# The last image's layers 2 and 3 written beside the end of the last but one's layer 3

## The chip, the cores and the metric

The kernel runs on one core of a Trainium2 chip. A core has TensorE (PE, matrix products into PSUM; its weight loads are shown as PEld), VectorE (DVE), ScalarE (ACT), GpSimd (POOL) and SyncE (SP), which issues most of the DMAs. Each engine works off its own queue. The metric is the device time of one execution in microseconds. Before the change it was 3833.54 us, the median of 3 runs (3829.8 to 3834.8).

## The reference, cut to what matters

Four residual layers run one after the other over x of shape (8, 384, 32, 32), each on a group-normalised input. All arithmetic is in f32.

```python
x = x + L0(_gn(x))   # depthwise 3x3, batch norm, attention with 8 heads
x = x + L1(_gn(x))   # 4 experts, top 2 routing, 384 -> 384 -> 384
x = x + L2(_gn(x))   # depthwise 3x3 with ternary weights, then 1x1 with ternary weights
x = x + L3(_gn(x))   # deformable attention, 6 heads
```

Layer 3 on one image:

```python
q = einsum('bchw,oc->bohw', x, q_w)
off = gelu(bn(conv5x5_stride2(q, groups=128)))         # depthwise, 3 groups of 128 channels
offset, modulation = 1x1(off)                          # tanh, sigmoid
x_s = grid_sample_bilinear(x, positions) * modulation  # 16 x 16 samples per group
k, v = einsum(x_s, kv_w)
out = softmax(q k^T / 8) v                             # 1024 queries, 256 keys
out = einsum(out, proj_w) + proj_b
```

From layer 1 on no image depends on another one. The layers of one image depend on each other.

## The kernel before, in words

An image is held as a tile of 128 partitions x 3 channel slices x 1024 pixels in f32 (`image`, five buffers). Layer 0 takes the first half of the run and isn't touched. The rest works image by image. `layer1` returns a list of 48 units, 24 for each half of 512 pixels: 12 hidden units (`hidden`, L1232: three products, a ReLU on ScalarE into a tile `hd0` to `hd11` at L1240, and a weighting on VectorE at L1218), then 12 output units (`result`, L1251), each of which adds the products of three hidden tiles into a bank. The fourth part of an output slice adds the bank to the image (L1257).

`layer2` and `layer3` are generators. They write out instructions, and at each `yield` they tell how long, in microseconds by the author's estimate, TensorE would have nothing to do. The loop at the end of the kernel sums these numbers and, whenever they reach `UNIT` (2.6), writes out one unit of the next image's layer 1:

```python
for stage in (layer2(pl, b, xt), layer3(pl, b, xt, put_image(b), False)):
    for idle in stage:
        due += idle
        while due >= UNIT and units:
            units.pop(0)()
            due -= UNIT
for u in units:
    u()
```

For the last image there are no units, so its layers 2 and 3 are written after all of the last but one's. The programming framework plans each engine's queue from what is written: what is written earlier goes first, but an instruction whose inputs are ready can go ahead of one that is still waiting. Once planned, a queue is worked off in its order.

`layer2` takes statistics (`gn_start`, L105), normalises them with two small products and a power on GpSimd (`gn_finish`, L116 to L132), applies them on ScalarE (`affine`, L146, into `h2`), and runs the 3x3 depthwise convolution as nine taps per channel slice (L1311 the first, L1320 the others) on VectorE. On the last image slice 0 runs on GpSimd instead (L1311, L1323, L1324: product into a temporary, then a sum). The 1x1 convolution is `pw` (L1341, 36 matmuls), added to the image at L1345 and stored at L1346.

`layer3` normalises again into `h3`, computes q (`pq`, L1367; copied out at L76 or L78 by turns of ScalarE and VectorE), transposes `h3` (`px`, L1379, copied into `xT`), runs the 5x5 convolution with stride 2 on VectorE (`off`, L1413 and L1415) and a GELU (L1420). Then come the offsets (`pom`, L1426 and L1427; L1430 to L1445), bilinear weights for eight row blocks (L1458 to L1460, the last on GpSimd) and sampling products (`xsb`, `xs`, L1464, L1471), k and v (`pk`, `pv`, L1478, L1487), six attention units (scores `s` L1504, exponentials L1511, pair sum on GpSimd L1535, `pav` L1520, `pss` L1546, and VectorE's transposes, reciprocal and product L1538 to L1557), and the projection (`pf`, L1609, added at L1613, stored at L1620).

[...]`big` is two tiles of two banks (pw, pq, px, pom, scores, projection), `vbank` is one bank (statistics, `xs2`, pav, pss), `fbank` is three single banks (layer 1).

Of the kernel before, what the change touches and what calls it, by code (L numbers as in the profile page):

```python
# [9 lines left out]
ALU = mybir.AluOpType  # L10
AX = mybir.AxisListType

B, C, H, W = 8, 384, 32, 32
N = H * W
P = 128
# [37 lines left out]
def tile_kernel(ctx: ExitStack, tc: tile.TileContext, i: dict, out: bass.AP):  # L53
# [10 lines left out]
    def big(name):  # L64
        return ps_big.tile([P, N], F32, tag="big", name=name)
# [71 lines left out]
    def gn_finish(st, tag, psum):  # L137

        return gn_scale(*gn_spread(gn_mean(st, tag), tag, psum), tag, psum)
# [5 lines left out]
    def affine(dst, src, ss):  # L145
        nc.scalar.activation(dst, src, AF.Identity, bias=ss[:, 1:2], scale=ss[:, 0:1])  # L146
# [1006 lines left out]

    xs_img, started = {}, {}

    def layer1(pl, b, late=False):


# [69 lines left out]
        def hidden(h, k):  # L1228
            e, dc = divmod(k, KC)
            ph = fbank(f"ph{b}_{h}_{k}")  # L1230
            for c in range(KC):
                nc.tensor.matmul(  # L1232
                    ph, lhsT=w1[:, e, c, dc * P : (dc + 1) * P], rhs=state["h1"][c],
                    start=(c == 0), stop=(c == KC - 1),
                )
            if late and h == 1:
                hd = spare(k)
            else:
                hd = pl.one([P, HALF], f"hd{k}", f"hd{b}_{h}_{k}")
# [56 lines left out]
        return units  # L1296

    def layer2(pl, b, xt):
        st = None
        for c in range(KC):  # L1300
            st = gn_start(xt, f"d2_{b}", c, st)
            yield 1.3
        ss = gn_finish(st, f"d2_{b}", vbank)
        yield 5.0
        h2, y = pl.img(f"h2_{b}"), pl.img(f"y_{b}")
        for c in range(KC):
            affine(h2[:, c, :], xt[:, c, :], ss)
        def taps(c, eng):
            src = h2[:, c, :].rearrange("p (h w) -> p h w", h=H)
            dst = y[:, c, :].rearrange("p (h w) -> p h w", h=H)  # L1310
            eng.tensor_scalar(dst, src, tap2[:, c, 4:5], None, ALU.mult)  # L1311
            yield 0.8
            for t in (0, 1, 2, 3, 5, 6, 7, 8):
                dy, dx = t // 3 - 1, t % 3 - 1
                r0, r1 = max(0, -dy), H - max(0, dy)
                c0, c1 = max(0, -dx), W - max(0, dx)
                d = dst[:, r0:r1, c0:c1]
                f = src[:, r0 + dy : r1 + dy, c0 + dx : c1 + dx]
                if eng is nc.vector:
                    eng.scalar_tensor_tensor(d, f, tap2[:, c, t : t + 1], d, ALU.mult, ALU.add)  # L1320
                else:
                    tmp = pl.flat([P, r1 - r0, c1 - c0], f"tap{t}_{b}")
                    eng.tensor_scalar(tmp, f, tap2[:, c, t : t + 1], None, ALU.mult)  # L1323
                    eng.tensor_tensor(d, d, tmp, ALU.add)  # L1324
                yield 1.25


        alone = b == B - 1
        for c in range(KC):
            if alone and c == 0:  # L1330
                for _ in taps(c, nc.gpsimd):
                    pass
            else:
                yield from taps(c, nc.vector)
        yield 2.0
        for m in range(KC):
            pw = big(f"pw{b}_{m}")
            for h in range(2):
                hs = slice(h * HALF, (h + 1) * HALF)
                for c in range(KC):  # L1340
                    nc.tensor.matmul(  # L1341
                        pw[:, hs], lhsT=upw2[:, c, m * P : (m + 1) * P], rhs=y[:, c, hs],
                        start=(c == 0), stop=(c == KC - 1),
                    )
            nc.vector.scalar_tensor_tensor(xt[:, m, :], pw, mp, xt[:, m, :], ALU.mult, ALU.add)  # L1345
            nc.sync.dma_start(out=x2_dram[b, :, m, :], in_=xt[:, m, :])  # L1346
            yield 0.0

    def layer3(pl, b, xt, put, general):

        st = None
        for c in range(KC):
            st = gn_start(xt, f"d3_{b}", c, st)
        yield 3.0
        ss = gn_finish(st, f"d3_{b}", vbank)
        yield 5.0
        h3 = pl.img(f"h3_{b}")
        for c in range(KC):
            affine(h3[:, c, :], xt[:, c, :], ss)
        yield 3.0  # L1360
        q = pl.img(f"q_{b}")
        for m in range(KC):
            pq = big(f"pq3_{b}_{m}")
            for h in range(2):
                hs = slice(h * HALF, (h + 1) * HALF)
                for c in range(KC):
                    nc.tensor.matmul(  # L1367
                        pq[:, hs], lhsT=wq3[:, c, m * P : (m + 1) * P], rhs=h3[:, c, hs],
                        start=(c == 0), stop=(c == KC - 1),
                    )  # L1370
            evac(q[:, m, :], pq)
            yield 0.0

        xT = pl.img(f"xT_{b}").rearrange("p c n -> p (c n)").rearrange("p (t c) -> p t c", t=NT8)
        for t in range(0, NT8, 2):
            px = big(f"px_{b}_{t}")
            for k in range(2):
                for c in range(KC):
                    nc.tensor.transpose(  # L1379
                        px[:, k * HALF + c * P : k * HALF + (c + 1) * P],  # L1380
                        h3[:, c, (t + k) * P : (t + k + 1) * P], ident,
                    )
            evac(
                xT[:, t : t + 2, :].rearrange("p t (q c) -> p t c q", c=KC),
                px.rearrange("p (t n) -> p t n", t=2)[:, :, :C].rearrange(
                    "p t (c q) -> p t c q", c=KC
                ),
            )
            yield 0.4

        off = pl.flat([P, NG, HS, HS], f"off_{b}")
        src = q.rearrange("p g (h w) -> p g h w", h=H)

        def span(s):
# [24 lines left out]
        offf = off.rearrange("p g h w -> p (g h w)")  # L1419
        nc.scalar.activation(offf, offf, AF.Gelu, bias=bo3, scale=so3)  # L1420
        yield 3.0

        om = []
        for r in range(3):
# [29 lines left out]
        for t in range(NT8):  # L1454
            i0, i1 = _sample_rows(t)
            sl = slice(i0 * HS, i1 * HS)
            wt = pl.flat([P, NG, (i1 - i0) * HS], f"wt_{b}_{t}")
            nc.scalar.activation(wt, gy3[:, :, sl], AF.Abs, bias=npos[:, t : t + 1])  # L1458
            nc.scalar.activation(wt, wt, AF.Relu, bias=1.0, scale=-1.0)
            nc.gpsimd.tensor_tensor(wt, wt, gx3[:, :, sl], ALU.mult)  # L1460
            if t == 0:
                yield 2.0
            for g in range(NG):
                nc.tensor.matmul(  # L1464
                    xps[g][:, sl], lhsT=xT[:, t, g * P : (g + 1) * P], rhs=wt[:, g, :],
                    start=False, stop=(t == NT8 - 1), skip_group_check=True,
                )
            yield 0.5
# [150 lines left out]
    def put_image(b):  # L1619
        return lambda m, xt: nc.sync.dma_start(out=out_img[b][:, m, :], in_=xt[:, m, :])  # L1620
# [23 lines left out]
    with pd:  # L1644
        for k, u in enumerate(units):
            u()
            if k == 8:
                tap2, upw2, mp, so3, bo3 = weights23(pl)
        for b in range(B):
            xt = xs_img.pop(b)  # L1650
            units = layer1(pl, b + 1) if b + 1 < B else []
            due = 0.0
            for stage in (layer2(pl, b, xt), layer3(pl, b, xt, put_image(b), False)):
                for idle in stage:
                    due += idle
                    while due >= UNIT and units:
                        units.pop(0)()
                        due -= UNIT
# [166 lines left out]
```

## Time and profile before

| what | us |
|---|---|
| median of 3 runs | 3833.54 |
| the profiled execution | 3834.06 |
| its span, first to last instruction | 3832.2 |
| TensorE busy in it | 3646.2 |
| VectorE busy in it | 1823.4 |
| GpSimd busy in it | 235.5 |
| mean granted TensorE clock | 0.975 |

Times in the views below are microseconds from the span's start unless marked ns. A line of groups or of waits names line, engine and tiles ("pw L1341 <- POOL y L1324" is a wait of the product pw for GpSimd's writing of y). The row of slices divides the span into 40 parts of 96 us; a digit is the busy share in tenths, and PEclk the granted clock in tenths of full speed. Matmuls of f32 show as two records each, so one unit of layer 1 is six.

### The profile page before, as it was taken

Reading aid. Unit: us, or ns where it says so; the run is one execution under the profiler, and the core shown is the slowest. Engines: PE = TensorE matmul, PEld = TensorE weight load, DVE = VectorE, ACT = ScalarE, POOL = GpSimd, SP = SyncE. Lnnn points to the kernel's source line nnn. Section 1 sums busy time; section 2 is a strip of 40 time slices with the busy share of each in tenths; the row PEclk is TensorE's granted clock in tenths of the full one; section 3 lists DMA queues with packets and bytes.
Section 4 is the critical chain, followed back from the end, with each engine's and each line's share of the span. In section 5 each row is a group of like instructions: output and inputs, shape, how many; then the busy total and the mean of one; then the engine's idle time right before and its main releaser. Section 6 shows DMA issues by size and latency. Waiting matters only on the chain.

```text
span 3832.2 us, 39353 instructions
## 1 busy us (share of the span) xinstructions
PE 3646.2 (95%) x15754; PEld 1520.9 (40%) x15754; DVE 1823.4 (48%) x2826; ACT 1314.7 (34%) x1557; POOL 235.5 (6%) x170
## 2 busy tenths in 40 slices
PE   7999899999999999999899999999999999999748
PEld 3444333333333333333344445444444444445213
DVE  5876223232323232332256665475656646565544
ACT  2222454554546353534112323223232222313102
POOL 0000000000000000000000100101011010100321
PEclk9999999999999999999899999999999999999868
DMA  6777211121202121111620000101001010010000
GB/s 200 245 235 241 100 53 43 53 61 40 74 24 72 27 69 38 59 49 50 233 81 33 17 33 19 48 17 33 33 17 34 17 50 17 25 42 1 17 17 18
DMA packets 83097, 242.64 MB, mean 63 GB/s; under 512 B 18336, under 2 KB 18864, under 8 KB 82520
## 3 DMA queue, kind: packets, MB, share of 16 engines
q1 hardware_dynamic: 69894, 200.56, 15.7%
q10 hardware_dynamic: 13008, 39.43, 3.0%
q8 instruction: 128, 2.10, 0.2%
q14 instruction: 67, 0.55, 0.0%
HBM read 122.78 MB, written 75.50 MB: 52 GB/s over the span
## 4 chain that ended last, share of the span: by engine, by line
PE 39%; DVE 9%; POOL 1%; issue 1%; ACT 1%; DVEq 0%; ACTq 0%; POOLq 0%
PE y L1251 10%; PE ph L1232 8%; DVE y L1320 5%; PE pq L1367 3%; PE pw L1341 3%; PE s L1504 3%; PE pf L1609 3%; PE pav L1520 2%; PE pss L1546 1%; DVE hd L1218 1%; DVE off L1415 1%; PE pk L1478 1%; PE xsb L1464 1%; PE pv L1487 1%; POOL tap L1323 1%
## 5 line engine op out<-in xcount | busy, mean ns | idle before, releaser
L630 ACT ACTIVATE p<-s 128x1024 f32<-128x1024 f32 x512 | 496.4, 1021 | 497.1 <-PE s L623 496.8
L1251 PE MATMUL y<-hd,w_sb 128*128 128x512 f32 x1080 | 493.4, 601 | 3.6 <-DVE hd L1218 3.6
L638 PE MATMUL pav<-p,vt 64*64 64x512 f32 x4096 | 486.4, 589 | 0.0
L1232 PE MATMUL ph<-h,w_sb 128*128 128x512 f32 x1104 | 483.6, 594 | 0.0
L623 PE MATMUL s<-qk,qk 48*64 48x512 f32 x3072 | 373.1, 600 | 4.4 <-ACT p L630 4.4
L381 PE MATMUL pk<-st,cw_sb 126*126 126x512 f32 x720 | 321.5, 608 | 3.6 <-DVE ga_a L118 3.3
L1232 PEld LDWEIGHTS ph<-h,w_sb 128*128 128x128 f32 x1104 | 207.8, 190 | 252.5 <-issue 249.4
L1251 PEld LDWEIGHTS y<-hd,w_sb 128*128 128x128 f32 x1080 | 198.8, 191 | 250.4 <-issue 236.3
L638 PEld LDWEIGHTS pav<-p,vt 64*64 64x64 f32 x4096 | 156.2, 133 | 285.3 <-issue 285.0
L595 DVE COPY ta<-pav 128x512 f32<-128x512 f32 x64 | 44.3, 692 | 439.1 <-PE pav L638 436.1
L1320 DVE SCALAR_TENSOR_TENSOR y<-h,tap,y 128x961 f32<-128x961 f32 (+1 forms) x184 | 233.5, 1295 | 1.6
L381 PEld LDWEIGHTS pk<-st,cw_sb 126*126 126x126 f32 x720 | 140.1, 197 | 177.7 <-issue 170.7
L1415 DVE SCALAR_TENSOR_TENSOR off<-q,dw_sb,off 128x225 f32<-128x225 f32 (+3 forms) x432 | 209.6, 542 | 1.9
L1240 ACT ACTIVATE hd<-ph,b_sb 128x512 f32<-128x512 f32 x180 | 122.6, 681 | 254.3 <-PE ph L1232 253.9
L623 PEld LDWEIGHTS s<-qk,qk 48*64 48x64 f32 x3072 | 102.6, 133 | 241.6 <-issue 184.7
L1341 PE MATMUL pw<-y,upw 128*128 128x512 f32 x288 | 128.6, 602 | 54.8 <-POOL y L1324 50.1
L78 DVE COPY qk<-pq 128x512 f32<-128x512 f32 x48 | 33.2, 692 | 293.1 <-PE pq L558 281.4
L387 ACT COPY y<-pk 126x512 f32<-126x512 f32 (+1 forms) x136 | 76.2, 583 | 254.4 <-DMA raw<-y 115.9
L1511 ACT ACTIVATE p<-s 128x1024 f32<-128x1024 f32 x96 | 93.0, 1021 | 171.8 <-PE s L1504 171.7
L146 ACT ACTIVATE h<-x,ss_d 128x1024 f32<-128x1024 f32 x42 | 49.6, 1231 | 287.6 <-DVE ss_d L132 287.6
L575 PE MATMUL po<-att,wo_sb 128*128 128x512 f32 x288 | 134.5, 617 | 9.5 <-DMA att<-al 9.5
L1218 DVE TENSOR_TENSOR hd<-hd,cb 128x512 f32<-128x512 f32 x180 | 122.9, 688 | 34.6 <-ACT hd L1240 34.2
(281 smaller groups left out, 4124.0 us busy)
## 6 DMA issues: line engine op xcount, KB each, us to landing
g<-raw SPq DMA_DIRECT2D x72, 512.0 KB
st<-pad SPq DMA_DIRECT2D x180, 168.0 KB
raw<-y ACTq DMA_DIRECT2D x180, 168.0 KB
xa<-in_x_dram SPq DMA_DIRECT2D x24, 512.0 KB
xh<-in_x_dram SPq DMA_DIRECT2D x48, 256.0 KB
f<-in_x_dram SPq DMA_DIRECT2D x24, 512.0 KB
f<-o SPq DMA_DIRECT2D x24, 512.0 KB
o<-ot SPq DMA_DIRECT2D x42, 256.0 KB
```

The source lines that it names most:

```text
L381: nc.tensor.matmul(pk[h].rearrange("p (h w) -> p h w", w=W)[: 3 * nch, :, o0 : o0 + c1 - c0], lhsT=lhs, rhs=rhs, start=(k == 0), stop=(k = ...
L575: nc.tensor.matmul(po, lhsT=wo0[:, c, m * P : (m + 1) * P], rhs=atts[b][:, c, hs], start=(c == 0), stop=(c == KC - 1),)
L623: nc.tensor.matmul(s[64 * k : 64 * k + 64, j * HALF : (j + 1) * HALF], lhsT=kt[r, k0 : k0 + 64], rhs=qt[r, h * HALF : (h + 1) * HALF], sta ...
L630: nc.scalar.activation(p, s, AF.Exp, scale=scale)
L638: nc.tensor.matmul(pav[k][64 * j : 64 * j + 64, :], lhsT=vts[b % 2][r, kc, 2 * hd : 2 * hd + 2, :].rearrange("p a b -> p (a b)"), rhs=p[r, ...
L1218: nc.vector.tensor_tensor(hd, hd, state["cb"], ALU.mult)
L1232: nc.tensor.matmul(ph, lhsT=w1[:, e, c, dc * P : (dc + 1) * P], rhs=state["h1"][c], start=(c == 0), stop=(c == KC - 1),)
L1240: nc.scalar.activation(hd, ph, AF.Relu, bias=b1[:, k : k + 1])
L1251: nc.tensor.matmul(y, lhsT=w2[:, e, dc, m * P : (m + 1) * P], rhs=state[h, k], start=(k == 0), stop=(k == NE * KC - 1),)
L1320: eng.scalar_tensor_tensor(d, f, tap2[:, c, t : t + 1], d, ALU.mult, ALU.add)
L1341: nc.tensor.matmul(pw[:, hs], lhsT=upw2[:, c, m * P : (m + 1) * P], rhs=y[:, c, hs], start=(c == 0), stop=(c == KC - 1),)
L1415: nc.vector.scalar_tensor_tensor(d, f, dw3[:, t : t + 1], d, ALU.mult, ALU.add)
```

## The change

The loop stops following the old scheme in the last but one image (image 6; the last is image 7). `layer3` gets a marker, `yield None`, right after the GELU of the offsets. At this marker in image 6 all remaining units of image 7's layer 1 are written out at once. Then the rest of image 6's layer 3 and the whole of image 7's layers 2 and 3 are written in turn: after each step of image 6, two steps of image 7. In the other images the marker does nothing.

For image 7 the tiles and banks are others: statistics, pw, pq and px use the three `fbank` banks in halves of 512 (or 384), where the other images use `big` and `vbank`; `y`, `h3` and `xT` lie in the tiles of layer 1's hidden values, and `off` in the tile `h1`. For this the twelve tiles `hd0` to `hd11` become four tiles of three slices each, in all images. The copies out of these banks, the affine into `h3` and the sums into the image are done in halves. The convolution of image 7's layer 2 has all three slices on VectorE.

```diff
+    def third(pl, k, name):
+        return pl.one([P, KC, HALF], f"hd{k}", name)
+
+    def pair(last, name):
+        if last:
+            return None, [fbank(f"{name}_{h}") for h in range(2)]
+        t = big(name)
+        return t, [t[:, :HALF], t[:, HALF:]]
...
-                hd = pl.one([P, HALF], f"hd{k}", f"hd{b}_{h}_{k}")
+                if k % 3 == 0:
+                    state["hd"] = third(pl, k // 3, f"hd{b}_{h}_{k}")
+                hd = state["hd"][:, k % 3, :]
...
     def layer2(pl, b, xt):
+        last = b == B - 1
...
-        ss = gn_finish(st, f"d2_{b}", vbank)
+        ss = gn_finish(st, f"d2_{b}", fbank if last else vbank)
...
+        if last:
+            y = [third(pl, c, f"y_{b}_{c}").rearrange("p a n -> p (a n)")[:, :N] for c in range(KC)]
...
-        alone = b == B - 1
-        for c in range(KC):
-            if alone and c == 0:
-                for _ in taps(c, nc.gpsimd):
-                    pass
-            else:
-                yield from taps(c, nc.vector)
...
-            pw = big(f"pw{b}_{m}")
+            whole, pw = pair(last, f"pw{b}_{m}")
...
+            outs = zip((xm[:, :HALF], xm[:, HALF:]), pw) if last else [(xm, whole)]
+            for d, f in outs:
+                nc.vector.scalar_tensor_tensor(d, f, mp, d, ALU.mult, ALU.add)
...
     def layer3(pl, b, xt, put, general):
...
+        if last:
+            h3 = [third(pl, h, f"h3_{b}_{h}") for h in range(2)]
+            for h in range(2):
+                for c in range(KC):
+                    affine(h3[h][:, c, :], xt[:, c, h * HALF : (h + 1) * HALF], ss)
...
+            whole, pq = pair(last, f"pq3_{b}_{m}")
...
+            if last:
+                for h in range(2):
+                    evac(q[:, m, h * HALF : (h + 1) * HALF], pq[h])
...
+            xT = [third(pl, 2 + h, f"xT_{b}_{h}").rearrange("p a n -> p (a n)") for h in range(2)]
...
+            off = pl.one([P, KC, HALF], "h1", f"off_{b}").rearrange("p c n -> p (c n)")
...
         nc.scalar.activation(offf, offf, AF.Gelu, bias=bo3, scale=so3)
         yield 3.0
+
+        yield None
...
+        def layers(b):
             xt = xs_img.pop(b)
+            yield from layer2(pl, b, xt)
+            yield from layer3(pl, b, xt, put_image(b), False)
+
+        for b in range(B - 1):
+            units = layer1(pl, b + 1)
             due = 0.0
+            this = layers(b)
+            for idle in this:
+                if idle is None:
+                    if b == B - 2:
+                        break
+                    continue
+                due += idle
+                while due >= UNIT and units:
+                    units.pop(0)()
+                    due -= UNIT
             for u in units:
                 u()
+
+        following = layers(B - 1)
+        for _ in this:
+            for _ in range(2):
+                next(following)
+        for _ in following:
+            pass
```

More of the change, by code (lines that the diff above doesn't have):

```diff
@@ L1302, in layer2 @@
             yield 1.3
-        ss = gn_finish(st, f"d2_{b}", vbank)
+        ss = gn_finish(st, f"d2_{b}", fbank if last else vbank)
         yield 5.0
-        h2, y = pl.img(f"h2_{b}"), pl.img(f"y_{b}")
+        h2 = pl.img(f"h2_{b}")
+        if last:
+            y = [third(pl, c, f"y_{b}_{c}").rearrange("p a n -> p (a n)")[:, :N] for c in range(KC)]
+        else:
+            y = pl.img(f"y_{b}")
+            y = [y[:, c, :] for c in range(KC)]
         for c in range(KC):
             affine(h2[:, c, :], xt[:, c, :], ss)
-        def taps(c, eng):
+        for c in range(KC):
             src = h2[:, c, :].rearrange("p (h w) -> p h w", h=H)
-            dst = y[:, c, :].rearrange("p (h w) -> p h w", h=H)
-            eng.tensor_scalar(dst, src, tap2[:, c, 4:5], None, ALU.mult)
+            dst = y[c].rearrange("p (h w) -> p h w", h=H)
+            nc.vector.tensor_scalar(dst, src, tap2[:, c, 4:5], None, ALU.mult)
             yield 0.8
@@ L1318, in taps @@
                 f = src[:, r0 + dy : r1 + dy, c0 + dx : c1 + dx]
-                if eng is nc.vector:
-                    eng.scalar_tensor_tensor(d, f, tap2[:, c, t : t + 1], d, ALU.mult, ALU.add)
-                else:
-                    tmp = pl.flat([P, r1 - r0, c1 - c0], f"tap{t}_{b}")
-                    eng.tensor_scalar(tmp, f, tap2[:, c, t : t + 1], None, ALU.mult)
-                    eng.tensor_tensor(d, d, tmp, ALU.add)
-                yield 1.25
-        alone = b == B - 1
-        for c in range(KC):
-            if alone and c == 0:
-                for _ in taps(c, nc.gpsimd):
-                    pass
-            else:
-                yield from taps(c, nc.vector)
+                nc.vector.scalar_tensor_tensor(d, f, tap2[:, c, t : t + 1], d, ALU.mult, ALU.add)
+                yield 1.25
         yield 2.0
         for m in range(KC):
-            pw = big(f"pw{b}_{m}")
+            whole, pw = pair(last, f"pw{b}_{m}")
             for h in range(2):
@@ L1341, in layer2 @@
                     nc.tensor.matmul(
-                        pw[:, hs], lhsT=upw2[:, c, m * P : (m + 1) * P], rhs=y[:, c, hs],
+                        pw[h], lhsT=upw2[:, c, m * P : (m + 1) * P], rhs=y[c][:, hs],
                         start=(c == 0), stop=(c == KC - 1),
                     )
-            nc.vector.scalar_tensor_tensor(xt[:, m, :], pw, mp, xt[:, m, :], ALU.mult, ALU.add)
-            nc.sync.dma_start(out=x2_dram[b, :, m, :], in_=xt[:, m, :])
+            xm = xt[:, m, :]
+            outs = zip((xm[:, :HALF], xm[:, HALF:]), pw) if last else [(xm, whole)]
+            for d, f in outs:
+                nc.vector.scalar_tensor_tensor(d, f, mp, d, ALU.mult, ALU.add)
+            nc.sync.dma_start(out=x2_dram[b, :, m, :], in_=xm)
             yield 0.0
     def layer3(pl, b, xt, put, general):
+        last = b == B - 1
         st = None
@@ L1354, in layer3 @@
         yield 3.0
-        ss = gn_finish(st, f"d3_{b}", vbank)
+        ss = gn_finish(st, f"d3_{b}", fbank if last else vbank)
         yield 5.0
-        h3 = pl.img(f"h3_{b}")
-        for c in range(KC):
-            affine(h3[:, c, :], xt[:, c, :], ss)
+        if last:
+            h3 = [third(pl, h, f"h3_{b}_{h}") for h in range(2)]
+            for h in range(2):
+                for c in range(KC):
+                    affine(h3[h][:, c, :], xt[:, c, h * HALF : (h + 1) * HALF], ss)
+        else:
+            t = pl.img(f"h3_{b}")
+            for c in range(KC):
+                affine(t[:, c, :], xt[:, c, :], ss)
+            h3 = [t[:, :, :HALF], t[:, :, HALF:]]
         yield 3.0
@@ L1362, in layer3 @@
         for m in range(KC):
-            pq = big(f"pq3_{b}_{m}")
+            whole, pq = pair(last, f"pq3_{b}_{m}")
             for h in range(2):
-                hs = slice(h * HALF, (h + 1) * HALF)
                 for c in range(KC):
                     nc.tensor.matmul(
-                        pq[:, hs], lhsT=wq3[:, c, m * P : (m + 1) * P], rhs=h3[:, c, hs],
+                        pq[h], lhsT=wq3[:, c, m * P : (m + 1) * P], rhs=h3[h][:, c, :],
                         start=(c == 0), stop=(c == KC - 1),
                     )
-            evac(q[:, m, :], pq)
-            yield 0.0
-        xT = pl.img(f"xT_{b}").rearrange("p c n -> p (c n)").rearrange("p (t c) -> p t c", t=NT8)
+            if last:
+                for h in range(2):
+                    evac(q[:, m, h * HALF : (h + 1) * HALF], pq[h])
+            else:
+                evac(q[:, m, :], whole)
+            yield 0.0
+        T2 = NT8 // 2
+        if last:
+            xT = [third(pl, 2 + h, f"xT_{b}_{h}").rearrange("p a n -> p (a n)") for h in range(2)]
+        else:
+            t = pl.img(f"xT_{b}").rearrange("p c n -> p (c n)")
+            xT = [t[:, : T2 * C], t[:, T2 * C :]]
+        xT = [t.rearrange("p (t c) -> p t c", t=T2) for t in xT]
         for t in range(0, NT8, 2):
-            px = big(f"px_{b}_{t}")
+            h, t2 = divmod(t, T2)
+            whole, px = pair(last, f"px_{b}_{t}")
             for k in range(2):
@@ L1379, in layer3 @@
                     nc.tensor.transpose(
-                        px[:, k * HALF + c * P : k * HALF + (c + 1) * P],
-                        h3[:, c, (t + k) * P : (t + k + 1) * P], ident,
-                    )
[L1383 to L1388, printed above, removed]
-            yield 0.4
-        off = pl.flat([P, NG, HS, HS], f"off_{b}")
+                        px[k][:, c * P : (c + 1) * P],
+                        h3[h][:, c, (t2 + k) * P : (t2 + k + 1) * P], ident,
+                    )
+            if last:
+                for k in range(2):
+                    evac(
+                        xT[h][:, t2 + k, :].rearrange("p (q c) -> p c q", c=KC),
+                        px[k][:, :C].rearrange("p (c q) -> p c q", c=KC),
+                    )
+            else:
+                evac(
+                    xT[h][:, t2 : t2 + 2, :].rearrange("p t (q c) -> p t c q", c=KC),
+                    whole.rearrange("p (t n) -> p t n", t=2)[:, :, :C].rearrange(
+                        "p t (c q) -> p t c q", c=KC
+                    ),
+                )
+            yield 0.4
+        if last:
+            off = pl.one([P, KC, HALF], "h1", f"off_{b}").rearrange("p c n -> p (c n)")
+            off = off[:, : NG * LS].rearrange("p (g h w) -> p g h w", g=NG, h=HS)
+        else:
+            off = pl.flat([P, NG, HS, HS], f"off_{b}")
         src = q.rearrange("p g (h w) -> p g h w", h=H)
@@ L1464, in layer3 @@
                 nc.tensor.matmul(
-                    xps[g][:, sl], lhsT=xT[:, t, g * P : (g + 1) * P], rhs=wt[:, g, :],
+                    xps[g][:, sl], lhsT=xT[t // T2][:, t % T2, g * P : (g + 1) * P], rhs=wt[:, g, :],
                     start=False, stop=(t == NT8 - 1), skip_group_check=True,
@@ L1648, in tile_kernel @@
                 tap2, upw2, mp, so3, bo3 = weights23(pl)
-        for b in range(B):
+        def layers(b):
             xt = xs_img.pop(b)
-            units = layer1(pl, b + 1) if b + 1 < B else []
+            yield from layer2(pl, b, xt)
+            yield from layer3(pl, b, xt, put_image(b), False)
+        for b in range(B - 1):
+            units = layer1(pl, b + 1)
             due = 0.0
[L1653 to L1658, printed above, removed]
+            this = layers(b)
[8 more added lines that the diff above has]
+                    due -= UNIT
             for u in units:
                 u()
+        following = layers(B - 1)
[4 more added lines that the diff above has]
+            pass
         okt = pl.flat([P, B * NU3 * 16], "okt3")
```

## The prediction

> **What bounds the kernel now.** I read the page first, then the chain that ended last, then waits and stretches of the tail. Engine totals and the row of slices:
>
> ```profile
> PE 3646.2 (95%) x15754; PEld 1520.9 (40%) x15754; DVE 1823.4 (48%) x2826; ACT 1314.7 (34%) x1557; POOL 235.5 (6%) x170
> PE   7999899999999999999899999999999999999748
> PEclk9999999999999999999899999999999999999868
> ```
>
> TensorE is busy nearly everywhere; the holes are the first slice and the last four. So a gain must come from TensorE's idle time at the end. The chain and the waits of the tail say what fills it (chain: start, length, what):
>
> ```profile
> 3580.82 35.49 issue
> 3617.13 1.25 ACT h L146
> 3618.47 2.85 POOL y L1311
> 3664.10 2.06 POOL y L1324
> 3666.20 17.41 PE pw L1341 x36
> 3690.88 18.72 PE pq L1367 x36
> 3739.76 1.03 ACT off L1420
> 3771.46 1.08 PE s L1504 x4
> 3810.74 13.95 PE pf L1609 x32
> PE pw L1341 <- POOL y L1324: 50.1, 1, 50.1
> PE pom L1426 <- ACT off L1420: 26.8, 1, 26.8
> ```
>
> Until 3612.5 TensorE is full ("issue" hides the back-to-back matmuls of image 6 and of layer 1 of image 7). After it only image 7 is left, a serial chain: 50.1 us for its depthwise convolution, which GpSimd's third ends last, and 26.8 us for the 5x5 convolution on VectorE. The chain of image 7 from the last layer-1 sum to the end is 3832.2 − 3612.5 = 219.7 us.
>
> The stretches (for the layer-1 output matmuls alone: us, PE busy (x), PEld busy (x), clock, DMA share, GB/s):
>
> ```profile
> 3510.00:3612.60 102.60, 33.45 (x72) 13.05 (x72) 1.00 0.04 16
> 3612.60:3833.00 220.40, 0.00 (x0) 0.00 (x0) 0.75 0.04 15
> ```
>
> 72 matmuls are 12 units; with two hidden units (L1232) 14 units of layer 1 lie after the point where image 6's offset GELU ends (3509.2). The new marker stands exactly there.
>
> **The change, step by step.** Times go on from 3509.9, where the old trace starts image 6's first offset matmul; everything ahead of it I cost at nothing.
>
> *Twelve hidden tiles become four of three (all images).* Same bytes, same instructions. A third comes free only when its three readers are done, but one output unit (L1251) reads exactly three, so it is one unit as before; and the next half writes there three units (3 x 2.58 us) later. Cover: those 7.7 us. Without it, the rival below. 0 us.
>
> *Units put first.* 14 units x 2.58 us (six matmuls in the chain's rows) = 36.1, so layer 1 of image 7 ends at 3546.0 instead of 3612.5: 66.5 us earlier. Nothing is removed from TensorE; the rest of image 6 (offsets, sampling, k and v, six attention units, projection) is what is late next, by 36 us, and it now lies beside image 7.
>
> *Normalisation of layer 2.* From the last y matmul (3612.5) to the first tap (3618.5) took 6.0; start of the taps 3552.0. Its tiny matmuls, the power on GpSimd and ScalarE's affine queue among image 6's offset work; up to 2 us, inside the range.
>
> *Convolution, 27 taps on VectorE.* Removed: 17 GpSimd instructions and eight temporaries. Added: 9 taps on VectorE. Alone a tap is 1.20 start to start in image 6's layer 2 (first tap 0.68), so 24 x 1.20 + 3 x 0.68 = 30.9. Image 6's VectorE work falls in between: position arithmetic and clears, about 3.0 of 4.5; sampled-value products 1.2; k copy 1.0: 5.2. Beside GpSimd the same taps are slower (ns min/median/max):
>
> ```profile
> L1320 DVE SCALAR_TENSOR_TENSOR y<-h,tap,y x24: 1205/1230/1252, 3394.9 to 3429.9; 128x961 f32<-128x961 f32 x12, 128x992 f32<-128x992 f32 x12
> L1320 DVE SCALAR_TENSOR_TENSOR y<-h,tap,y x16: 1205/1930/3254, 3620.3 to 3649.8; 128x961 f32<-128x961 f32 x8, 128x992 f32<-128x992 f32 x8
> ```
>
> Sixteen taps lost 29.9 − 16 x 1.21 = 10.5 us in some 31 us of busy GpSimd, a third of its time. [...]GpSimd still has image 6's eight weight products (0.6 each) and two pair sums (2.35 each) here, 9.5 us: [...]by the row 3.3. I take the row. Conv ends at 3552.0 + 30.9 + 5.2 + 3.3 = 3591.4.[...]
>
> Image 6's attention meets this: its scores could start about 26 us after 3546 (24.5 when warm with its units taken out, 30.7 in image 7), at 3572. Its first VectorE transpose is written after 26 of the 27 taps. VectorE's queue is not the written order (statistics of image 7 ran at 3543.37, long before their turn), but I read it as earliest-written first among what is ready, so the transpose waits until near 3591; the one bank for pav/pss is held, and TensorE idles some 9 us.
>
> *pw.* 36 matmuls: 15.5 warm (15.45 for pf in the chain), 17.4 cold here before. I take 17.5, plus 3.0 of attention ahead of it: 3611.9. Its six half evacuations (three whole ones before, 1.28 each) hide behind 2.58 us of matmuls per half.
>
> *Second normalisation.* pw's end to pq's start was 3690.88 − 3683.6 = 7.3. Halves save about 1; queueing behind a pair sum on GpSimd (2.35) or an attention step costs as much. 7.3: 3619.2.
>
> *pq* 15.5 warm (18.7 before) + 3.0 of attention: 3637.7; last half copy 0.7: 3638.4. xT in eight copies instead of four is beside it.
>
> *5x5 convolution.* Alone 25.8 + 0.6 = 26.4. On VectorE beside it: half the xT copies, 4 x 0.65 = 2.6; some 3.5 attention units at 0.72 + 0.72 + 0.26 + 1.73 + 0.71 = 4.1, 14.5; two projection sums 2.6. Sum 46.1: 3684.5. Check by load: VectorE has about 114 us of work from 3546 on and idles some 24 us while pw and pq hold TensorE: 3684.
>
> *Rest of image 7.* From the GELU (3739.76) to the end 92.4, unchanged: 3776.9. A warm TensorE would shorten it: sampling steps are 1.28 apart here and 0.67 in image 6, held to 0.85 by ScalarE's two instructions per step; pk took 5.80 against 3.88: about 6 in all with pom. [...]By my times image 6's projection ends near 3673, 11 us before pom: [...]by image 6's rows 86.4. [...]the granted clock was 0.70 in the old stretch from 3740 to 3771.
>
> *DMAs.* Three stores of image 7's layer-2 output (10.6 us on SP's queue) go ahead of image 6's three output stores, not behind. Nothing waits for either: image 7's attention tile finds another of the five image buffers free. 0 us; if it did wait, about 10.
>
> Sum: 3776.9 − 3832.2 = −55.3. The profiled execution took 3834.1, which is 1.9 outside its span and 0.5 above the median: 3833.5 − 55.3 = 3778.2. Because the six VectorE multiplies are slow only when they meet GpSimd (0.69 against 2.1), I round down to 3777.
>
> **Rivals.**
>
> *Better packing.* VectorE hardly idles: attention of image 6 slips in ahead of the taps and under pw and pq. Then its 114 us follow 3552 without holes: 3666, and 92.4 less 3 for a warmer start: 3755 with what lies outside the span: about 3757. For it: TensorE was 99% busy from 3380 to 3510 with the same mixing. Against: VectorE had little to do there during its matmuls.
>
> *Queues in each other's way.* The order of each queue is fixed beforehand, and a tap or a pair sum lies ahead of what TensorE needs. Six attention units and twelve half evacuations late by one tap each (1.2 to 2.2): 18 x 1.7 = 30, so 3807. For it: GpSimd's neighbour effect above. Against: three banks give 5 us of slack per half.
>
> *It doesn't do what it says.* Image 7 needs a buffer (h2's or a third) that image 6 frees only at its end; then the chain starts near 3597 as before and only the convolution is shorter, 46.7 to 31: 3818. Against: five image buffers hold xt, q, xT (later attention) of image 6, xt and h2 of image 7, which is just five.
>
> *Slower.* The thirds make the layer-1 stream stop at the start of each half in all images: if the first hidden activation had to wait until the whole group was read, through VectorE's weighting and back. 16 halves; it must cost over 55 / 16 = 3.5 us each to decide, and at 4.1 gives 3843. For it: TensorE is the bound there, so every stop counts in full. Against: in the old trace pq starts (3690.88) when the first of three affine slices of one tile is done, so parts of a tile are waited for one by one.
>
> **How the numbers follow.** Likeliest case 0.60, 3777, its own range 3762 to 3795. Better packing 0.18, 3757 with ends 3742 to 3762. Queues in the way 0.13, 3807 (3795 to 3815). No overlap 0.04, 3818. Slower 0.05. The range 3746 to 3806 leaves out about half of the queue case, the last two and the best end of the packing. Faster 0.93; within 0.2% (7.7 us, about what can be told from no change here) 0.02, which are weak forms of the last two; slower 0.05.
>
> **What would show it.** Right: TensorE's granted clock near 1.0 until about 3670; the wait of pw for GpSimd gone; pw near 3591, pq near 3619, the last offset GELU near 3684, then 92 us; taps between 1.2 and 2.2. A hole in TensorE before pw and none later would fit my reading of the queue. Wrong: time already shifted before 3510 (the thirds), [...]pw well before 3585 (better packing), or pq waiting for VectorE evacuations.

## The result and the profile after

The new kernel takes 3772.31 us, the median of 4 runs (3772.12 to 3774.23), against 3832.85 us before in the same comparison: ratio 0.9844, 95% interval 0.9827 to 0.9861. That is 60.5 us less; 56.5 were predicted. A second series gave 3775.15 us and 0.9849 (0.9832 to 0.9865).

The profiled execution of the new kernel has a span of 3770.3 us. About 4.1 of the 61.9 us between the two spans aren't the change's. The same hidden unit of layer 1 ahead of the changed tail starts at 3480.28 instead of 3484.36, and the first score product of layer 0, whose code is the same, at 415.6 instead of 419.8. This start moves by some us from run to run (417.8 in the profile of the kernel with thirds alone, 419.1 in a second one of the new kernel). The tail itself gained 57.8 us.

Engine totals, TensorE's busy slices and the granted clock, from the page of the new kernel:

```profile
PE 3647.7 (97%) x15754; PEld 1521.3 (40%) x15754; DVE 1818.9 (48%) x2841; ACT 1316.8 (35%) x1564; POOL 194.8 (5%) x153
PE   7999899999999999999799999999999999999898
PEclk9999999999999999999899999999999999999898
```

TensorE does the same work (3647.7 against 3646.2 us); the 7, 4 and 8 at the end have become 8, 9 and 8. The chain that ended last, in order of time (start, length, what):

```profile
3511.18 30.90 PE y L1265 x72
3542.07 0.86 PE pom L1467 x2
...
3548.54 1.25 ACT h L146
3549.81 0.76 DVE y L1331
...
3569.94 4.67 PE pw L1347 x6
...
3601.87 5.36 PE pw L1347 x12
...
3615.23 10.50 PE pq L1384 x24
...
3678.06 1.03 ACT off L1459
3679.14 2.08 PE pom L1467 x2
```

Layer 1 of image 7 runs through at once, its layer 2 starts at 3548.5 instead of 3617.1, and its last GELU ends 61.7 us earlier. What TensorE waits for from 3542 to the end (us in total, times, longest):

```profile
PE xsb L1505 <- POOL wt L1501: 12.3, 2, 7.9
PE pom L1467 <- ACT off L1459: 6.7, 1, 6.7
PE pw L1347 <- DVE y L1339: 3.0, 1, 3.0
```

The 50.1 us for the convolution and the 26.8 us ahead of image 7's offsets have become 3.0 and 6.7. The longest single wait, 7.9 us, is new: image 6's sampling waits for its bilinear weights, and no layer-1 unit is left to fill the hole. Image 7's three affines (3.5 us, from 3548.5) stand ahead of these weights on ScalarE; without such a neighbour the same wait is 4.4 us in image 7.

### The profile page after: what moved, and what is told of

Read it like the earlier page. It is cut to its first block, busy times and chain, and to the rows that moved or that the text cites. A ratio compares the mean times of both kernels' runs of the same rounds, so it can differ in the third digit from the quotient of the medians.

```text
span 3770.3 us, 39346 instructions
## 1 busy us (share of the span) xinstructions
PE 3647.7 (97%) x15754; PEld 1521.3 (40%) x15754; DVE 1818.9 (48%) x2841; ACT 1316.8 (35%) x1564; POOL 194.8 (5%) x153
## 3 DMA queue, kind: packets, MB, share of 16 engines
q1 hardware_dynamic: 69894, 200.56, 16.1%
## 4 chain that ended last, share of the span: by engine, by line
PE 40%; DVE 9%; ACT 1%; issue 0%; POOL 0%; DVEq 0%; POOLq 0%; ACTq 0%
PE y L1265 11%; PE ph L1244 8%; DVE y L1339 6%; PE pq L1384 3%; PE pw L1347 3%; PE pf L1650 3%; PE s L1545 3%; PE pav L1561 2%; PE pss L1587 1%; DVE hd L1230 1%; DVE off L1454 1%; PE pk L1519 1%; PE pv L1528 1%; PE xsb L1505 1%; PE plog L1007 1%; PE pom L1467 1%
## 5 line engine op out<-in xcount | busy, mean ns | idle before, releaser
L1339 DVE SCALAR_TENSOR_TENSOR y<-h,tap,y 128x992 f32<-128x992 f32 (+1 forms) x192 | 233.8, 1241 | 1.6
L558 PE MATMUL pq<-g,wq_sb 128*128 128x512 f32 x288 | 132.8, 612 | 2.2 <-ACT g L483 2.2
```

The costliest lines, as they stand in the source:

```text
L558: nc.tensor.matmul(pq, lhsT=w_in[v][:, c, pr * P : (pr + 1) * P], rhs=acts[b][v][:, c, h * HALF : (h + 1) * HALF], start=(c == 0), stop=(c ...
L1339: nc.vector.scalar_tensor_tensor(d, f, tap2[:, c, t : t + 1], d, ALU.mult, ALU.add)
```

## The experiments

"From layer 1's end" below counts from the end of the last y product of image 7, so that the moving start of layer 0 drops out. For the new kernel the span's end lies 228.2 us after it (219.7 before the change), and the GELU of image 7's 5x5 convolution starts 136.0 after it. These stage times are from one profile of each kernel; two profiles of the new kernel, whose spans differ by 3.2 us, give 228.2 and 228.3 (experiment 9).

**1. The convolution alone.** The kernel before, with

```diff
-            if alone and c == 0:
+            if False:
```

> The kernel before, with all three slices of the last image's 3x3 convolution on VectorE and nothing else changed. If the gain comes from starting image 7 some 66 us earlier (my theory): the convolution shrinks from 47.7 us (3618.5 to 3666.2) to about 31, nothing else moves, so 16 to 17 us less than before, 3816 us. If most of the gain comes from taking GpSimd away from VectorE's side (rival): more than half of it, 3803 us or less.

Measured 3809.55 us, ratio 0.9944 (0.9927 to 0.996), 22.3 us less than the 3831.84 beside it. Its chain has the piece:

```profile
3644.47 14.12 PE pw L1341 x28
```

From the affine to the last tap it takes 31.9 us instead of 49.1 (17.2 less), as expected. Two things I had not counted come on top. Eight of the 36 pw records run before the last tap, since slice 0, the first that pw adds, is no longer the last to be ready: pw's time behind the convolution is 14.1 instead of 17.4. And pq takes 17.2 instead of 18.7. From layer 1's end it is 198.9 us. The rival (more than half of the gain) is out.

**2. The thirds alone.** The kernel before, with

```diff
-                hd = pl.one([P, HALF], f"hd{k}", f"hd{b}_{h}_{k}")
+                if k % 3 == 0:
+                    state["hd"] = pl.one([P, KC, HALF], f"hd{k // 3}", f"hd{b}_{h}_{k}")
+                hd = state["hd"][:, k % 3, :]
```

> The kernel before, with the twelve hidden tiles of layer 1 made into four tiles of three slices and nothing else changed. My theory: no effect, within 5 us of before. Rival (the grouping makes layer 1 wait at each half): at least 2 us for each of 16 halves, 32 us slower. That part of the new kernel's gain lies here is a third reading: then 4 us or more faster.

Measured 3831.27 us, ratio 1.0001 (0.9992 to 1.001, 12 runs). The grouping costs nothing and gains nothing.

**3. The overlap with slice 0 on GpSimd.** The new kernel, with

```diff
-            nc.vector.tensor_scalar(dst, src, tap2[:, c, 4:5], None, ALU.mult)
-            yield 0.8
+            eng = nc.gpsimd if last and c == 0 else nc.vector
+            eng.tensor_scalar(dst, src, tap2[:, c, 4:5], None, ALU.mult)
+            if eng is nc.vector:
+                yield 0.8
...
+                if eng is nc.gpsimd:
+                    tmp = pl.flat([P, r1 - r0, c1 - c0], f"tap{t}_{b}")
+                    eng.tensor_scalar(tmp, f, tap2[:, c, t : t + 1], None, ALU.mult)
+                    eng.tensor_tensor(d, d, tmp, ALU.add)
+                    continue
```

> The new kernel, with slice 0 of the last image's 3x3 convolution put back on GpSimd. My theory: GpSimd's slice takes 47 us or more as before, so the convolution ends 13 us or more later than the 34.4 us that it took in the new kernel, and the eight weight products of image 6 queue on the same engine: 3785 to 3805 us. Rival (inside the overlap nobody waits for the convolution, since TensorE has image 6's work): 3776 us or less.

Measured 3806.69 us, ratio 0.9933 (0.9916 to 0.9951): 34 us slower than the new kernel, a little above what was expected. TensorE's waits say why it is more than the convolution's own delay:

```profile
PE xsb L1512 <- POOL wt L1508: 48.9, 1, 48.9
PE pw L1354 <- POOL y L1344: 0.5, 1, 0.5
```

Image 6's bilinear weights stand behind slice 0 in GpSimd's queue, so image 6 stops too, and its sampling, k, v and attention then run into pw and pq. The parts don't add: the convolution alone gains 22.3, the overlap without it 25.2, both together 60.5.

**4. Without image 6's attention.** The new kernel, with

```diff
-        att = pl.img(f"att3_{b}")
+        skip = b == B - 2
+        att = q if skip else pl.img(f"att3_{b}")
...
-        if not general:
+        if skip:
+            nc.vector.memset(rec3[:, b * NU3 : (b + 1) * NU3, :], 1.0)
+            for _ in range(14):
+                yield 1.0
+        elif not general:
```

> The new kernel without the six attention units of image 6 (its projection reads q in the place of the attention's result; all else is there). My theory charges these units with 3.0 us at pw, 3.0 at pq and 14.5 us of VectorE's time beside the 5x5 convolution: about 20 us less, 3752 us. If they only fill holes of image 7's chain (rival): within 6 us of the new kernel, 3766 to 3775.

Measured 3744.99 us, 27.3 less than the new kernel (29.1 from layer 1's end). So the six units do lie on image 7's chain. What is left, 199.1 us from layer 1's end, is what image 7 took with nothing of image 6 beside it in experiment 1 (198.9). By stage (us, new kernel and without):

| stage of image 7 | with | without | charged | shown |
|---|---|---|---|---|
| last tap to pw's end | 23.0 | 11.1 | 3.0 | 11.9 |
| pw's end to pq's start | 8.0 | 5.8 | 0 | 2.2 |
| pq | 16.9 | 15.7 | 3.0 | 1.2 |
| pq's end to the GELU | 46.0 | 31.4 | 14.5 | 14.6 |

The edit also lets image 6's projection start earlier: six of its products move between pw and pq, and one of its three sums (1.3 us on VectorE) leaves the last stage. So the last row holds some 13 us of attention.

**5. One step of image 7 for each of image 6.** `range(2)` becomes `range(1)` in the last loop.

> The new kernel with one step of image 7 after each step of image 6 instead of two, so image 6 goes ahead. If image 7's chain sets the end (my theory), what lies ahead of it counts: attention of image 6 pushes taps and pw back, 8 to 16 us slower than the new kernel, 3780 to 3788 us. If VectorE's load sets the end, whatever the order (rival): within 4 us of 3772.

Measured 3799.76 us, 0.9911 (0.9895 to 0.9928). The order counts, and for more than I expected. The chain of this kernel:

```profile
3624.35 13.93 PE pf L1650 x32
3638.28 14.61 PE pw L1347 x34
```

The taps end at 3598.7, but pw stands behind all of image 6's attention and its projection in TensorE's queue, and starts in earnest 39.6 us later. VectorE's load was the same (1824.0 us busy against 1818.9).

**6. Three steps, up to image 7's marker.**

```diff
+        going = True
         for _ in this:
-            for _ in range(2):
-                next(following)
+            for _ in range(3):
+                if going:
+                    going = next(following) is not None
```

> The new kernel with three steps of image 7 after each step of image 6, up to image 7's own marker. Theory: less of image 6's attention (measured at 27 us for all six units) lies ahead of image 7's pw, and some of it comes to lie beside image 7's offsets and sampling, where TensorE has holes: 6 to 14 us less, 3758 to 3766 us. Rival (VectorE's load): within 4 us of 3772. What could spoil it: image 6's attention then delays image 7's own, 3776 us or more.

Measured 3779.15 us, 0.9861 (0.9844 to 0.9877); from layer 1's end 230.9, so 2.7 more than the new kernel. By the runs the two can't be told apart clearly (the intervals overlap), but the gain that the theory expected isn't there. The GELU comes 11.0 us earlier, as the theory says (pw ends 12.4 us sooner), but the offset products start 16.1 us after the GELU does (1.1 in the new kernel):

```profile
3672.97 11.37 PE pf L1650 x26
...
3685.70 1.12 PE pom L1467 x2
```

Image 6's projection is ahead of them in the queue. I had named a spoiler of this kind, but had looked for it in image 6's attention.

**7. The marker behind image 6's offsets.** `yield None` stands after `yield 6.0`, ahead of `xsb`.

> The new kernel with the marker behind the offsets of image 6 (after its three tanh and the position arithmetic are written) instead of ahead of them, so that image 6's offset products go ahead of the remaining units. It takes away the 8 us hole of TensorE before image 6's sampling and starts image 7 about 4 us later. If image 7's chain sets the end (theory): 4 us later start, paid back in part by attention of image 6 being out of the way of pw, 3770 to 3778 us. If TensorE's holes are what is lost (rival): 8 us less, 3764 us.

Measured 3776.85 us, 0.9853 (0.9836 to 0.9869), inside what the theory gave. From layer 1's end it is 227.3. TensorE's waits:

```profile
PE pom L1465 <- ACT off L1459: 15.3, 1, 15.3
PE pw L1347 <- DVE y L1339: 10.9, 1, 10.9
PE xsb L1504 <- POOL wt L1500: 4.4, 1, 4.4
```

The hole of 7.9 us ahead of image 6's sampling is gone (the 4.4 is image 7's), and the holes ahead of pw and of image 7's offsets grew by 7.9 and 8.6. The rival, 8 us less, is out. But the edit doesn't show what filling a hole alone is worth: image 6 now stands further ahead when the turns begin, so its scores start at 3572.7 instead of 3583.4, and image 7's pw ends 8 us later from layer 1's end.

**8. The clock kept up.** Eleven products whose result nobody reads:

```diff
+        if last:
+            wm = fbank("warm_a")
+            for _ in range(5):
+                nc.tensor.matmul(wm, lhsT=wq3[:, 0, :P], rhs=offf[:, :HALF], start=True, stop=True)
         gy, gx, md = om
...
             put(m, xt)
+            if b == B - 2 and m == KC - 1:
+                wm = fbank("warm_b")
+                for _ in range(6):
+                    nc.tensor.matmul(wm, lhsT=wq3[:, 0, :P], rhs=xt[:, m, :HALF], start=True, stop=True)
```

> The new kernel with eleven products added whose result nobody reads: six behind image 6's last sum, ahead of image 7's offset products, and five behind those, so that TensorE isn't idle there. If the last stage is slow because the granted clock fell (theory): offset products 1.5 us shorter, sampling steps 0.85 to 0.9 apart instead of 1.28 (3 us), pk 3.9 instead of 5.75: 5 to 7 us less, 3766 us. If ScalarE and GpSimd pace the sampling (rival): 3 us less at most, 3769 us or more.

Measured 3767.10 us, 0.9827 (0.9811 to 0.9844). From layer 1's end 220.6, 7.6 less than the new kernel; all of it lies behind the GELU (84.6 us to the end instead of 92.2). The stage from image 7's offset products to its scores, for the new kernel and for this one (window, length, busy us and records of PE, PEld, DVE, ACT, POOL, granted clock, DMA share, GB/s):

```profile
3679.10:3710.00 30.90, 26.23 (x92) 20.33 (x94) 6.08 (x11) 10.06 (x23) 4.35 (x8) 0.72 0.00 1
```

```profile
3681.80:3707.00 25.20, 23.94 (x109) 15.69 (x108) 5.99 (x11) 11.65 (x25) 4.36 (x8) 1.00 0.00 1
```

The sampling steps stand 0.67 apart instead of 1.28, and pk takes 4.12 instead of 5.75. The rival (ScalarE and GpSimd pace the sampling) is out for image 7.

**9. The new kernel again**, beside the next two.

> The new kernel once more, beside the two kernels below. 3772 us, within 4.

Measured 3775.15 us; from layer 1's end 228.3.

**10. Three steps, past the marker.** The last loop has `for _ in range(3): next(following, None)`.

> The new kernel with three steps of image 7 after each step of image 6, past image 7's marker too, so that image 7's offset products are written ahead of image 6's projection. In the run with three steps up to the marker, image 7's offset GELU ended 10 us earlier than in the new kernel (3668 against 3678), but its offset products then stood 16 us behind image 6's work in TensorE's queue. If that place in the queue is what ate the gain (theory): the products start within 2 us of the GELU, image 6's projection (15.5 us) moves into image 7's sampling and attention, part of it into holes: 3762 to 3770 us. Rival (image 7's chain is held by the load of its neighbour, wherever that stands): 3775 us or more, as with the marker.

Measured 3782.37 us, 0.9871 (0.9854 to 0.9887): by the medians 7.2 us slower than the new kernel beside it (the intervals overlap), and my theory fell. The offset products now start 3.8 us after the GELU's start, and the GELU is 9.3 us earlier, yet from layer 1's end it is 235.0, 6.8 more. From the GELU to the end it takes 108.3 instead of 92.2. The chain (this view ends at 3725, inside the last piece):

```profile
3700.87 5.15 PE pf L1650 x12
3706.02 1.08 PE s L1545 x4
...
3720.75 4.56 PE pf L1650 x10
```

Image 6's projection now cuts in three times (from 3700.7, 3720.8 and 3732.1), 5.3 or 5.4 us each (15.9 to 16.2 us, against 16.1 lost), ahead of and between the units of image 7's attention, where TensorE has no room: before the change it was busy 36.36 of 39 us there. The rival was right: the neighbour's work costs also here. Of the orders tried, two steps cost least; they leave the projection beside the 5x5 convolution, where TensorE waits for VectorE.

**11. The same with five unread products** between image 7's offsets and its sampling (the first part of experiment 8's change).

> The kernel with three steps past the marker, and five products that nobody reads between image 7's offsets and its sampling. Theory: the hole of TensorE there is 4.4 us, after which the sampling ran at a lower clock; filled, the steps are 0.67 apart instead of 1.28 and pk is 3.9 us: 4 to 7 us less than without them, 3757 to 3765 us. If image 6's work already fills that hole (rival): no gain, or 4 us lost.

Measured 3775.39 us, 7.0 less than experiment 10 beside it (5.0 less from layer 1's end), as the clock theory says (granted clock 1.00 instead of 0.74 from 3680 to 3700), and no better than the new kernel. The range expected (3757 to 3765) was missed, because experiment 10, from which it was counted, took 3782 and not the 3762 to 3770 expected. The hole that the products fill was 2.8 us in experiment 10, not 4.4: there the first sampling steps still stood 0.7 apart, the last ones 1.3.

**12. One hole only.** The new kernel with the first part of experiment 8's change alone.

> The new kernel with only the five unread products between image 7's offsets and its sampling (the hole of 4.4 us), without the six ahead of the offsets. With eleven, the stage from the offset GELU to the end took 84.6 us instead of 92.2. If the hole of 4.4 us alone keeps the sampling at the lower clock (theory): the offsets stay slow (about 1.5 us), sampling steps 0.67 apart and pk 3.9: 86 us from the GELU, 3768 us. If the hole ahead of the offsets is what counts (rival): less than 3 us gained, 3772 us or more.

Measured 3771.11 us, 0.9844 (0.983 to 0.9857). By the runs this can't be told from the new kernel. In the profile the stage behaves as expected: 86.1 us from the GELU to the end, 222.2 from layer 1's end, against 92.2 and 228.2. The offset products are still slow (the first pair 2.08 us, as in the new kernel), and the sampling steps are 0.68 apart. So the hole of 4.4 us between offsets and sampling holds 6 of the 7.6 us, the one ahead of the offsets the rest.

Of the kernels that do the whole work, experiment 8 has the lowest median. Its interval overlaps that of the new kernel, so that it beats it rests on the stage times more than on the medians.

## Why the prediction was right

The times of the sum, beside those of the new profile with 4.1 us added for what moved ahead of the tail:

| step | predicted | measured + 4.1 |
|---|---|---|
| layer 1 of image 7 ends | 3546.0 | 3546.2 |
| first tap | 3552.0 | 3553.9 |
| last tap ends | 3591.4 | 3588.3 |
| pw ends | 3611.9 | 3611.3 |
| pq starts | 3619.2 | 3619.3 |
| 5x5 convolution starts | 3638.4 | 3637.1 |
| GELU | 3684.5 | 3682.2 |
| end | 3776.9 | 3774.4 |

- **Units first, thirds at nothing:** right, the first to 0.2 us, the second by experiment 2.
- **Normalisation:** 7.7 us instead of 6.0. VectorE's position arithmetic of image 6 stands between the small steps, which was allowed for in the range.
- **Convolution:** too long by 5.0 us. Of the 5.2 us of image 6's work, the position arithmetic was done before the first tap. The neighbour was put at 3.3, from the row of the old taps. What remains above the taps' own 30.9 us is 3.5, of which products and k copy fill about 1.9; so VectorE lost some 1.6, beside the eight weight products alone (the two pair sums came after the last tap). But that isn't all that the two engines cost each other. I had charged VectorE alone; GpSimd's eight products took 11.5 us instead of 5.0. My reading did not have that, and it slowed image 6's sampling, as the next point says.
- **The hole ahead of pw:** wrong in its place and its cause. I had image 6's scores start at 3572 and then wait for the taps, with TensorE idle 9 us on the held bank. They started at 3583.4 (3587.5 with the shift), after the last tap began; TensorE idled 7.9 us ahead of image 6's sampling instead, and 3.0 ahead of pw. Two things made the scores late. Behind the hole the sampling went in steps of 1.5 us, the pace of GpSimd's weights beside the taps: they start at 3555.09, 3556.55 and 3558.05, the steps that wait for the ones before them at 3555.18, 3556.65 and 3558.14. (The granted clock was 0.50 there as well, but image 7's steps, at 0.51 from 3689.5 to 3700, are 1.28 apart.) And the sampling's VectorE products waited 7 us behind taps, from 3566.9 to 3573.9.
- **Attention ahead of pw and pq:** 3.0 and 3.0 were charged; experiment 4 shows 11.9 at pw, 2.2 behind it, 1.2 at pq. This is the term that was mis-sized. It didn't show in the sum, because other errors stood against it. Too little were 8.9 us for attention at pw and 1.9 for the start of the taps. Too much were 5.0 for the convolution and 6.4 for pw itself: without attention it ends 11.1 us after the last tap (experiment 4) and not 17.5, since eight of its 36 records run ahead of the last tap and the other 28 take 0.43 us each (the old ones 0.48). That pw's end was met to 0.6 us is luck; the middle of the sum is right in its total and not in its parts.
- **Beside the 5x5 convolution:** 14.5 charged, some 13 shown (14.6 with the projection sum that left the stage).
- **Rest of image 7:** 92.4 predicted, 92.2 measured. I had taken the old stretch, at a granted clock of 0.70, and not image 6's rows, and that held (0.72 from 3679.1 to 3710): TensorE idled 6.7 us ahead of the offset products (11 were expected), and the first pair took 2.08 us, at a clock of 0.50 (3679.1 to 3681.1), instead of 0.86. Experiments 8 and 12 show that the low clock is the cause, and what image 6's rows were worth: 86.4 was worked out from them, 84.6 was measured, since ScalarE doesn't hold the steps to 0.85 (they stood 0.67 apart).
- **Rivals:** the slower case fell with experiment 2. "It doesn't do what it says" put the convolution alone at 3818; it is 3810. Queues in each other's way is in part what the two-step order does too: attention cost 29.1 us and not the 20.5 charged. With one step it costs 27 us more, and with three it delays the offsets. Better packing was sought in experiments 6, 7 and 10 and not found.
- **Signs:** the wait of pw for GpSimd went, and the GELU and the end came where they were said to. Two signs failed. The granted clock was not near 1.0 until 3670 (0.50 from 3555 to 3570). And pw's first eight records ran at 3574, well before 3585, which was to speak for better packing; but the other 28 came after the last tap, so the sign was badly chosen.

That the 60.5 us exceed the tail's 57.8 by 3 is within the scatter of the runs; no run isolates it.

## What to carry to other kernels

Where the end of this kernel was one serial chain, moving its start earlier paid only in part, because the work that it overtook came to lie beside it. Image 7 starts 66 us earlier; with the convolution on VectorE in both kernels (experiment 1 and the new one) 37 us of that are left, and the other 29 are image 6's attention (experiment 4). Where the chain waited for another engine, the overtaken work cost what it took of that engine (some 13 us of VectorE beside the 5x5 convolution); where the chain itself filled TensorE, it cost its full length (15.9 to 16.2 us of projection, 16.1 lost, experiment 10). Compare orders by where the chain's own instructions stand in each queue, and not by the holes that are left. Five unread matmuls in an idle time of 4.4 us, behind which the sampling had run at a granted clock of 0.51, took 6 us off the last stage in the profile (experiment 12).

## What the runs showed of the hardware

- VectorE and GpSimd side by side: both gave way, and here GpSimd more. Groups of GpSimd's bilinear weights of image 6, in the new kernel beside the taps and in the old one without them (busy us, mean ns, idle before):

```profile
L1501 POOL TENSOR_TENSOR wt<-wt,om 128x192 f32<-128x192 f32 x6 | 9.0, 1526 | 0.0
```

```profile
L1460 POOL TENSOR_TENSOR wt<-wt,om 128x192 f32<-128x192 f32 x6 | 4.0, 676 | 2.6 <-ACT wt L1459 2.5
```

  One product takes 1.53 us instead of 0.68, while the nine taps that lie beside them took 1.50 each on average instead of 1.23. In the old tail, with GpSimd busy all the time, the taps went from 1.23 to 1.93 us in the median. There GpSimd paid too: its product took 3.61 us beside the taps and 2.74 after the last of them had ended (3651.7).

```profile
3648.70 3.61 POOL tap L1323
...
3654.37 2.74 POOL tap L1323
```

- The granted clock was 0.50 from 3555 to 3570 in the new kernel, behind an idle time of 7.9 us, although TensorE was busy 11.86 of these 15 us with sampling (steps of six short matmuls) and pw:

```profile
3555.00:3570.00 15.00, 11.86 (x49) 10.89 (x49) 15.00 (x12) 3.05 (x10) 10.41 (x8) 0.50 0.01 2
```

  Five matmuls of 512 columns in the 4.4 us ahead of image 7's sampling kept the steps at 0.68 us instead of 1.28 (experiment 12, granted clock 0.92 from 3680.7 to 3705); with six more ahead of the offsets the granted clock was 1.00 through the stage, from 3681.8 to 3707 (experiment 8).

- TensorE did not pass what stood first in its queue in experiment 5: image 7's taps end at 3598.7, and TensorE idled 0.90 us ahead of an attention product at 3623.27, until VectorE had written `tu`; the 34 records of pw came only at 3638.12, behind the projection.
